# Reordering the banded coefficients of an outlook attention stage by heads, with a copy on ScalarE

## Chip, cores and metric

The kernel runs on one core of a Trainium2 chip, in one launch. The metric is device time in microseconds (us). The kernel before took 2922.51 us, the median of three runs (2905.18, 2922.51 and 2929.6).

The core's engines run side by side, each through its own instructions in a fixed order: TensorE (PE in the profile; its weight loads stand apart as PEld), VectorE (DVE), ScalarE (ACT), GpSimd (POOL) and SyncE (SP), which here issues DMA transfers. A tile of 128 partitions in SBUF is the unit of data; PSUM is where TensorE writes.

## What is computed

The network has two layers on an input of 4 images of 32 x 32 pixels with 384 channels. Layer 0 is a gated attention and a mixture of experts; layer 1 is an "outlook" attention and a feed-forward network whose weights are Kronecker products. The change touches the outlook attention alone. Everything is fp32.

```
v    = x @ Wv                                    # 12 heads of 32 channels
a    = (x @ Wa).reshape(b, n, 12, 9, 9)          # 9 x 9 coefficients for each pixel and head
attn = softmax(a * d ** -0.5, axis=-1)
out[n, h, p] = sum_q attn[n, h, p, q] * v[neighbour q of n, h]   # a 3 x 3 neighbourhood
y    = fold(out)                  # each of the 9 outputs p is added at neighbour p of n
x    = x + y @ Wo
```

Unfolding and folding together mean that the output at a pixel is a weighted sum of v over a 5 x 5 neighbourhood, with one weight for each of 25 offsets and 12 heads.

## The kernel before

**The stage.** `outlook` (L1630) works through 32 tiles of 128 pixels, 8 tiles an image (tile o = 8 b + t). For each tile there are three steps, called at different turns of one loop over 41 steps.

- `scores` (L1721 on), at step o: the normalized tile is transposed on TensorE (`ps_tr`, copied to `xnT` by ScalarE at L151), multiplied by `wa` into 972 coefficients (`ps_a`, L1728, six matmuls of 128x486), turned into a softmax (maximum and subtraction on VectorE, L1737 and L1738; exp on ScalarE, L1743; sums, reciprocal and three multiplications on VectorE, L1745 to L1752), and multiplied by `wv` into `v` (`ps_v` L1772, copied by ScalarE at L1776). Four DMAs on SyncE (L1764 to L1769) move the coefficients of the upper and lower row of the neighbourhood by one image row into the tiles `up` and `down`.
- `band`, at step o + 2: the shifted coefficients are summed in `u` (two ScalarE copies, L1785 and L1786; three VectorE additions), shifted sideways by three matmuls (`ps_c` L1793), masked on VectorE into `co` (L1801), and written by a DMA (L1808, `room<-co`) into a zeroed place in DRAM from which one more DMA (L1814, `band<-room`, 1560 KB) reads a skewed copy: `band[p, t, h]` is the weight with which pixel p of the tile adds to pixel p + t - 66 before or behind it, for t in 0..259 and the 12 heads h. The heads lie innermost.
- `gather`, at step o + 5 (`LAG` is 3): for every head one matmul with `v` of that head as the weights (128 x 32) and `band[:, j : j + n, h]` as the moving operand (128 x n), n being 260, 194 or 66 where an image half cuts the band. Elements of one head are 12 floats (48 bytes) apart. The four heads of a group write four strips of 32 partitions of one PSUM bank, so that four matmuls can run side by side; the three groups have the banks `ys[0]` to `ys[2]`. An image has ten such sets of twelve matmuls, since the tiles t = 3 and t = 4 serve both halves of the image: t = 3 is used once more, with t = 4, when the second half begins. After the last tile of a half, ScalarE copies the three banks to `y` (L1839), and `mix` multiplies by `wo` (`ps_wo` L1846) and adds to x.

**What sets the order.** The order on SyncE and GpSimd is that of the program text. On TensorE, VectorE and ScalarE a scheduler puts the instructions in order when the kernel is built; on the chip each engine keeps to that order. Waits are semaphores that the framework places; a pool's buffer is given again only when its last reader is through. Pools that matter here: `ol_band` (five buffers for `band`; two for `yt`), `ol_ps_m` (two PSUM banks that `ps_tr`, `ps_v` and `ps_wo` share), and one bank each for `ys[0]` to `ys[2]`.

**After the stage** the feed-forward network (`Kron.run`) begins once the last tiles of the last image are mixed.

Of the kernel before, what the change touches and what calls it, by code (L numbers as in the profile page):

```python
# [10 lines left out]
FP = mybir.dt.float32  # L11
# [5 lines left out]
P = 128  # L17
# [4 lines left out]
KC = C // P  # L22
NH, HD = 12, 32
# [18 lines left out]
BAND = P + 2 * REACH  # L42
# [1587 lines left out]
def outlook(net, wv, wa, wo, left, router, kron, loads):  # L1630
# [10 lines left out]
    tc, nc = net.tc, net.nc  # L1641
# [4 lines left out]
    with ExitStack() as ctx:  # L1646
# [2 lines left out]
        mp = ctx.enter_context(tc.tile_pool(name="ol_moved", bufs=4, reuse_waits="tile"))  # L1649
        ap_ = ctx.enter_context(tc.tile_pool(name="ol_attn", bufs=3, reuse_waits="tile"))  # L1650
        vp = ctx.enter_context(tc.tile_pool(name="ol_v", bufs=7, reuse_waits="tile"))
        bp = ctx.enter_context(tc.tile_pool(name="ol_band", bufs=5, reuse_waits="tile"))
        ps_m = ctx.enter_context(tc.tile_pool(name="ol_ps_m", bufs=2, space=PSUM, reuse_waits="tile"))
        ps_a = ctx.enter_context(tc.tile_pool(name="ol_ps_a", bufs=1, space=PSUM, reuse_waits="tile"))
        ps_c = ctx.enter_context(tc.tile_pool(name="ol_ps_c", bufs=1, space=PSUM, reuse_waits="tile"))
# [4 lines left out]
        for dx in (-1, 0, 1):  # L1660
            m = const.tile([P, P], FP, name=f"shift_{dx}", tag=f"shift_{dx}")
# [41 lines left out]
                )  # L1703
            net.measure(work, i, net.x(i))

        attn, vs, bands, ys, moved = {}, {}, {}, {}, {}

        def room(b, t):

# [68 lines left out]
        def band(b, t):  # L1778


            H3 = 3 * H6
            u = work.tile([P, 6, 5, H3], FP, name="u", tag="u")
            down, up = (m.rearrange("p (g y e) -> p g y e", g=6, y=3) for m in moved.pop((b, t)))
            own = attn.pop((b, t))[:, 1].rearrange("p s x (y e) -> p (s x) y e", y=3)
            nc.scalar.copy(u[:, :, 0, :], down[:, :, 0, :])  # L1785
            nc.scalar.copy(u[:, :, 4, :], up[:, :, 2, :])  # L1786
            nc.vector.tensor_tensor(u[:, :, 1:3, :], down[:, :, 1:3, :], own[:, :, 0:2, :], ALU.add)
            nc.vector.tensor_tensor(u[:, :, 3, :], own[:, :, 2, :], up[:, :, 1, :], ALU.add)
            nc.vector.tensor_tensor(u[:, :, 2, :], u[:, :, 2, :], up[:, :, 0, :], ALU.add)
            pc = ps_c.tile([P, 512], FP, name="ps_c", tag="c")  # L1790
            grid = pc[:, : 5 * R].rearrange("p (s y e) -> p s y e", s=2, y=5)
            for qj in (1, 0, 2):
                nc.tensor.matmul(  # L1793
                    grid[:, :, :, (2 - qj) * H6 : (5 - qj) * H6],
                    lhsT=shift[qj - 1],
                    rhs=u.rearrange("p (s x) y e -> p s x y e", s=2)[:, :, qj, :, :],
                    start=qj == 1, stop=qj == 2, skip_group_check=True,
                )
            co = work.tile([P, 5, 5, NH], FP, name="co", tag="co", bufs=3)
            for hh in range(2):  # L1800
                nc.vector.tensor_tensor(  # L1801
                    co[:, :, :, hh * H6 : (hh + 1) * H6],
                    grid[:, hh].rearrange("p y (x h) -> p y x h", x=5),
                    inside.rearrange("p (x h) -> p x h", x=5).unsqueeze(1).to_broadcast([P, 5, 5, H6]),
                    ALU.mult,
                )
            room = net.room[t]
            nc.sync.dma_start(  # L1808
                out=room.rearrange("(p r) -> p r", p=P)[:, : 5 * IMG * NH]
                .rearrange("p (y r) -> p y r", y=5)[:, :, :R],  # L1810
                in_=co.rearrange("p y x h -> p y (x h)"),
            )
            m = bands[b, t] = bp.tile([P, BAND, NH], FP, name="band", tag="band")
            nc.sync.dma_start(  # L1814
                out=m.rearrange("p t h -> p (t h)"),
                in_=room[: P * BAND * NH].rearrange("(p r) -> p r", p=P),
            )

        def gather(b, half, t):

            first, last = (0, 4) if half == 0 else (3, 7)
            lo = max(P * t - REACH, 512 * half)
            hi = min(P * t - REACH + BAND, 512 * half + 512)
            j = lo - (P * t - REACH)
            for c in range(KC):
                if t == first:
                    ys[c] = ps_y.tile([P, 512], FP, name=f"ps_y{c}", tag=f"y{c}")
                for n in range(4):
                    h = 4 * c + n
                    nc.tensor.matmul(  # L1830
                        ys[c][32 * n : 32 * n + 32, lo - 512 * half : hi - 512 * half],
                        lhsT=vs[b, t][:, h * HD : (h + 1) * HD],
                        rhs=bands[b, t][:, j : j + hi - lo, h],
                        start=t == first, stop=t == last, skip_group_check=True,
                    )
            if t == last:
                y = work.tile([P, KC, 512], FP, name="y", tag="y", bufs=1)
                for c in range(KC):
                    nc.scalar.copy(y[:, c, :], ys[c])  # L1839
                return y  # L1840
# [14 lines left out]
        def at(step, f, *args):  # L1855
            later.setdefault(step, []).append((f, args))

        LAG = 3
        made = {}

        def gathered(b, half, t):
            y = gather(b, half, t)
            if y is not None:
                made[b, half] = y
# [4 lines left out]
        for b in range(B):  # L1869
            for t in range(NB):  # L1870
                o = b * NB + t
                at(o + 2, band, b, t)
                at(o + 2 + LAG, gathered, b, 0 if t < 5 else 1, t)
                if t == 4:
                    at(o + 2 + LAG, gathered, b, 1, 3)
                    at(o + 2 + LAG, gathered, b, 1, 4)
            for half in range(2):
                done = b * NB + (4 if half == 0 else 7) + 2 + LAG
                for n in range(4):
                    at(done + 1 + n // 2, mixed, b, half, n)  # L1880
        assert left[0] >= 2 * NB
        t_kron, first = 0, left[0]
        for step in range(B * NB + 9):
            b, t = divmod(step, NB)
# [207 lines left out]
def metaformer_kernel(  # L2092
# [19 lines left out]
    def rest(router, done):  # L2112

        with ExitStack() as late:
# [30 lines left out]
            with tc.manual_schedule(engines={eng.SP, eng.Pool}):  # L2145
                outlook(net, wv, wa, wo, range(done, NT), router, kron, loads)
# [85 lines left out]
```

## Time and profile before

| | |
|---|---|
| median of three runs | 2922.51 us |
| the profiled execution | 2919.42 us, its span 2917.6 us |
| the outlook stage | from about 2340 to 2820 us of the span |
| PE busy | 2761.2 us, 95% |
| DVE, ACT, POOL busy | 1347.7, 1207.3, 400.6 us |
| mean granted TensorE clock | 0.965 |
| banded matmuls (L1830) | 960 records, 102.7 us |

The profile is one execution. A row of a group has the line, the engine, the operation, the tiles written and read, the shapes and the count; then busy time in us, the mean duration of one in ns, and the idle time before them with what ended it. Each fp32 matmul of the program shows as two records, and the durations of matmuls overlap, so that the busy time of a group is less than count times mean. Times of a timeline are us from the span's start.

### The profile page before, as it was taken

How to read it: one execution, taken by the hardware profiler on the slowest of the kernel's cores; microseconds unless marked ns; L12 is line 12 of the kernel's file. 1: busy time of each engine (PE TensorE's matmuls, PEld its weight loads, DVE VectorE, ACT ScalarE, POOL GpSimd, SP SyncE). 2: the span in 40 equal slices, each digit the busy share in tenths (PEclk: the TensorE clock that was granted, in tenths of full speed). 3: DMA queues.
4: the chain of work that ended last, by engine and by line, in shares of the span. 5: the costliest groups of instructions: out<-in, count | busy, mean ns of one | idle time of the engine just before them, and what ended most of it. 6: DMA issues, size and time to landing. Idle time of an engine off the chain costs nothing. (4 is left out here: it accounts for less than half of the span.)

```text
span 2917.6 us, 36735 instructions
## 1 busy us (share of the span) xinstructions
PE 2761.2 (95%) x13236; PEld 1505.9 (52%) x13236; DVE 1347.7 (46%) x3714; ACT 1207.3 (41%) x2023; POOL 400.6 (14%) x499
## 2 busy tenths in 40 slices
PE   6989999999999998699999999999999998999988
PEld 4333333333334332267777777777777754444432
DVE  1376667777777776533000001111111146877642
ACT  3788677677768775211111211211211122122125
POOL 1000000110030004123111122122221101100000
PEclk9999999999999988699999999999999999999999
DMA  5143335223322234345454455555655437544432
GB/s 103 39 115 91 89 90 139 66 62 78 100 55 62 78 79 124 112 163 217 161 195 179 174 203 191 213 201 204 222 190 214 154 130 224 192 154 158 151 105 89
DMA packets 216992, 405.92 MB, mean 139 GB/s; under 512 B 83504, under 2 KB 177904, under 8 KB 203744
## 3 DMA queue, kind: packets, MB, share of 16 engines
q1 hardware_dynamic: 185504, 189.20, 21.6%
q0 software_dynamic: 27152, 209.66, 20.8%
q10 hardware_dynamic: 4144, 4.61, 0.5%
q8 instruction: 107, 1.75, 0.2%
q14 instruction: 85, 0.70, 0.1%
HBM read 305.35 MB, written 49.99 MB: 122 GB/s over the span
## 5 line engine op out<-in xcount | busy, mean ns | idle before, releaser
L1604 ACT ACTIVATE h<-ps_h,up 128x256 f32<-128x256 f32 x420 | 198.6, 473 | 915.2 <-PE ps_h L1600 915.1
L1600 PE MATMUL ps_h<-xbT,up 128*128 128x256 f32 x2520 | 553.2, 380 | 2.6 <-ACT h L1604 1.8
L1617 PE MATMUL ps_y<-down,h 128*128 128x384 f32 x1680 | 554.9, 488 | 0.0
L1600 PEld LDWEIGHTS ps_h<-xbT,up 128*128 128x128 f32 x2520 | 480.7, 191 | 76.7 <-ACT h L1604 2.7
L678 DVE CUSTOM_DVE_ANT_0 e<-e,rz,inv 128x1024 f32<-128x1024 f32 x384 | 475.2, 1274 | 30.0 <-DMA rz<-r_row 30.0
L626 ACT ACTIVATE e<-ps_s,shift 128x1024 f32<-128x1024 f32 x384 | 408.6, 1109 | 81.2 <-PE ps_s L616 48.7
L1617 PEld LDWEIGHTS ps_y<-down,h 128*128 128x128 f32 x1680 | 318.0, 191 | 206.6 <-issue 1.8
L1622 DVE TENSOR_TENSOR y<-ps_y,down 128x384 f32<-128x384 f32 x70 | 39.0, 558 | 721.1 <-PE ps_y L1617 721.1
L616 PE MATMUL ps_s<-q,k 32*128 32x512 f32 x1536 | 279.0, 664 | 36.4 <-ACT e L626 26.7
L634 PE MATMUL ps_o<-e,wv 128*32 128x512 f32 x1536 | 228.4, 670 | 39.3 <-DVE wv L685 36.7
L634 PE MATMUL ps_z<-e,rt_ones 128*32 128x512 f32 x1536 | 218.6, 643 | 0.0
L705 POOL DMA_DIRECT2D q<-po x96 | 76.1, 875 | 958.4 <-DMA q<-po 600.5
L366 ACT ACTIVATE below<-tk_left,tk_bound 128x1024 bf16<-128x1024 f32 (+1 forms) x160 | 184.3, 1152 | 38.0 <-DVE tk_bound L372 31.7
L1728 PE MATMUL ps_a<-wa,xnT 128*128 128x486 f32 x384 | 170.6, 594 | 8.9 <-DVE attn L1738 7.1
L616 PEld LDWEIGHTS ps_s<-q,k 32*128 32x128 f32 x1536 | 84.1, 189 | 168.7 <-ACT e L626 82.6
L281 PE MATMUL ps_t<-xnT,wqkv 128*128 128x512 f32 x288 | 135.4, 611 | 1.1 <-ACT q L520 0.7
L634 PEld LDWEIGHTS ps_o<-e,wv 128*32 128x32 f32 x1536 | 31.7, 112 | 200.3 <-issue 72.6
L1728 PEld LDWEIGHTS ps_a<-wa,xnT 128*128 128x128 f32 x384 | 73.1, 196 | 95.6 <-issue 87.1
L634 PEld LDWEIGHTS ps_z<-e,rt_ones 128*32 128x32 f32 x1536 | 52.7, 118 | 131.1 <-issue 127.1
L1830 PE MATMUL ps_y<-band,v 128*32 128x194 f32 (+2 forms) x960 | 102.7, 516 | 7.2 <-DMA band<-room 6.9
L1569 DVE SCALAR_TENSOR_TENSOR x<-yt,weight,x 128x384 f32<-128x384 f32 x38 | 23.5, 619 | 185.4 <-DMA x<-x 184.7
L1483 POOL DMA_INDIRECT yt<-yg,index x64 | 65.7, 1027 | 304.6 <-DVE x L1569 139.9
(345 smaller groups left out, 2859.2 us busy)
## 6 DMA issues: line engine op xcount, KB each, us to landing
band<-room SPq DMA_DIRECT2D x32, 1560.0 KB
rz<-r_row SPq DMA_DIRECT2D x48, 512.0 KB
yg<-y SPq DMA_DIRECT2D x70, 192.0 KB
q<-q SPq DMA_DIRECT2D x192, 64.0 KB
k<-k SPq DMA_DIRECT2D x192, 64.0 KB
room<-none SPq DMA_DIRECT2D x64, 192.0 KB
x<-x SPq DMA_DIRECT2D x38, 192.0 KB
o<-in_x_dram SPq DMA_DIRECT2D x33, 192.0 KB
```

The lines of the kernel that those rows point to most:

```text
L281: nc.tensor.matmul(ps, lhsT=lhsT(k), rhs=rhs(k), start=k == 0, stop=k == KC - 1)
L366: nc.scalar.activation(junk[:n], left[:n], AF.Sign, bias=bound[:n], accum_out=over[:n])
L616: nc.tensor.matmul(ps[:, half * 512 : half * 512 + 512], lhsT=self.k4[r, u * P : (u + 1) * P], rhs=self.q4[r, :], start=True, stop=True,)
L626: nc.scalar.activation(e, ps, AF.Exp, bias=shift, scale=QK_SCALE)
L634: nc.tensor.matmul(ps[r : r + 32, :], lhsT=lhsT(odd), rhs=self.es[2 * u + odd][:, half * 512 : half * 512 + 512], start=u == 0, stop=u == ...
L678: nc.vector.tensor_tensor_reduce(self.es[m], self.es[m], self.rz, 1.0, self.im["inv"][:, m, self.h : self.h + 1], ALU.mult, ALU.add, self. ...
L705: nc.gpsimd.dma_start(out=there, in_=po[r : r + 32, :], accum_op=ALU.add)
L1600: nc.tensor.matmul(ps, lhsT=up[:, o : o + P], rhs=xbT[:, k, :], start=k == 0, stop=k == KC - 1,)
L1604: nc.scalar.activation(h, ps, AF.Gelu, bias=up[:, KC * HID + f : KC * HID + f + 1])
L1617: nc.tensor.matmul(ps, lhsT=hs[f][:, t * P : (t + 1) * P], rhs=down[:, f * C : (f + 1) * C], start=f == 0, stop=f == NF - 1,)
L1728: nc.tensor.matmul(pa[:, hh, :HW_], lhsT=xnT[:, k, :], rhs=wa[:, k, hh * HW_ : (hh + 1) * HW_], start=k == 0, stop=k == KC - 1,)
L1830: nc.tensor.matmul(ys[c][32 * n : 32 * n + 32, lo - 512 * half : hi - 512 * half], lhsT=vs[b, t][:, h * HD : (h + 1) * HD], rhs=bands[b, t ...
```

## The change

ScalarE copies each landed band into a second tile `own` in which the heads are outermost, and the banded matmuls read that. The copy is three instructions, one for each group of four heads, of 4 x 260 = 1040 elements in each partition: it reads elements 48 bytes apart and writes elements that lie side by side. In the program text it stands at step o + 4, one before the gather. The buffers change with it: three for the landed band (five before) and two for the copy. `sort` stands at L1819 to L1825 of the changed kernel; what follows it moves down by eight or nine lines (the banded matmul is L1838 there).

```diff
-        bp = ctx.enter_context(tc.tile_pool(name="ol_band", bufs=5, reuse_waits="tile"))
+        bp = ctx.enter_context(tc.tile_pool(name="ol_band", bufs=1, reuse_waits="tile"))
...
-            m = bands[b, t] = bp.tile([P, BAND, NH], FP, name="band", tag="band")
+            m = landed[b, t] = bp.tile([P, BAND, NH], FP, name="band", tag="band", bufs=3)
...
+        def sort(b, t):
+
+            m = landed.pop((b, t))
+            own = bands[b, t] = bp.tile([P, NH, BAND], FP, name="own", tag="own", bufs=2)
+            for c in range(KC):
+                heads = slice(4 * c, 4 * c + 4)
+                nc.scalar.copy(own[:, heads, :], m[:, :, heads].rearrange("p t h -> p h t"))
...
-                        rhs=bands[b, t][:, j : j + hi - lo, h],
+                        rhs=bands[b, t][:, h, j : j + hi - lo],
...
                 at(o + 2, band, b, t)
+                at(o + 1 + LAG, sort, b, t)
                 at(o + 2 + LAG, gathered, b, 0 if t < 5 else 1, t)
```

More of the change, by code (lines that the diff above doesn't have):

```diff
@@ L1704, in add @@
             net.measure(work, i, net.x(i))
-        attn, vs, bands, ys, moved = {}, {}, {}, {}, {}
+        attn, vs, landed, bands, ys, moved = {}, {}, {}, {}, {}, {}
         def room(b, t):
```

## The prediction

> **What bounds the kernel now.** I read first the busy time by stretches of the span, to see which engine the outlook stage waits for; its columns are the stretch, its length, then for PE, PEld, DVE, ACT and POOL the busy us and instructions, the clock, DMA share and GB/s.
>
> ```profile
> 2460.00:2500.00 40.00, 38.40 (x207) 20.09 (x200) 31.91 (x80) 10.38 (x18) 9.83 (x10) 1.00 0.76 231
> ...
> 2580.00:2620.00 40.00, 40.00 (x200) 19.68 (x199) 27.27 (x67) 7.10 (x14) 0.00 (x0) 1.00 0.46 156
> 2620.00:2660.00 40.00, 40.00 (x165) 19.37 (x160) 28.51 (x72) 8.64 (x18) 0.72 (x2) 1.00 0.47 157
> 2660.00:2700.00 40.00, 40.00 (x232) 19.69 (x224) 29.63 (x82) 12.00 (x22) 0.00 (x0) 1.00 0.46 153
> ...
> 2780.00:2820.00 40.00, 32.33 (x238) 16.01 (x236) 17.37 (x44) 6.85 (x12) 0.00 (x0) 0.91 0.50 173
> ```
>
> From 2540 to 2784 TensorE never idles, VectorE works 70% and ScalarE 20% to 30%. There a shorter matmul shortens the stage. At both ends TensorE idles: transfers and chains bound it.
>
> Second, the groups of instructions by shape, from 2420 to 2815 (the last row is from the page's list of groups):
>
> ```profile
> L1846 PE MATMUL ps_wo<-wo,y 128*128 128x384 f32 x168 | 57.7, 491 | 0.0
> ...
> L1830 PE MATMUL ps_y<-band,v 128*32 128x260 f32 x384 | 56.1, 628 | 2.8 <-DMA band<-room 2.8
> ...
> L150 PE MATMUL ps_tr<-ident,xn 128*128 128x128 f32 x75 | 12.7, 276 | 0.7 <-DVE x L1850 0.7
> ...
> L1830 PE MATMUL ps_y<-band,v 128*32 128x66 f32 x192 | 8.8, 295 | 0.2 <-ACT y L1839 0.2
> ...
> L634 PE MATMUL ps_o<-e,wv 128*32 128x512 f32 x1536 | 228.4, 670 | 39.3 <-DVE wv L685 36.7
> ```
>
> A banded column costs (628 - 295) / (260 - 66) = 1.72 ns; a column that streams side by side (491 - 276) / (384 - 128) = 0.84 ns. The last row, of the same 128*32 form but contiguous, takes 670 ns for 512 columns, where 1.72 ns a column would make some 1060. So the 48-byte step is the cause, and it costs a factor of 2.05.
>
> Third, the timeline of ScalarE and SyncE around one tile, and the chain of waits at the end:
>
> ```profile
> 2597.22 1.01 ACT L1743 ACTIVATE attn<-attn 128x972 f32<-128x972 f32 x1 [0.47 <-DVE attn L1738]
> ...
> 2613.16 1.01 ACT L1743 ACTIVATE attn<-attn 128x972 f32<-128x972 f32 x1 [0.25 <-DVE attn L1738]
> 2619.66 0.48 ACT L151 COPY xnT<-ps_tr 128x384 f32<-128x384 f32 x1 [5.48 <-PE ps_tr L150]
> ```
>
> ```profile
> 2620.03 0.54 SPq L1764 DMA_DIRECT2D up<-attn  x1
> ...
> 2622.57 0.53 SPq L1808 DMA_DIRECT2D room<-co  x1
> 2624.99 0.33 SPq L1814 DMA_DIRECT2D band<-room  x1
> ```
>
> ```profile
> 2807.64 6.32 DMA band<-room
> 2814.00 2.22 PE ps_y L1830 x24
> ```
>
> The exp of a tile ends at 2614.17; SyncE issues that tile's moves at 2620.03, behind them the band of two tiles before at 2624.99, and a band lands 6.32 us after its issue: 2631.3, 17.1 us after the exp. This loop matters below.
>
> **The change part by part.** All sums are made against the profiled execution, 2919.42 us (its span 2917.6 and 1.8 around it), 0.1% under the median of the three runs.
>
> TensorE. The four strips of a set run side by side, so a run of banded matmuls lasts as long as its fullest strip. In the built order of before there are 48 such runs with 53,504 columns in the fullest strips (two records a matmul): 92.0 us at 1.72, and the remaining 10.7 of the measured 102.7 are 0.22 a run for starting and draining. In the built order of the changed kernel the scheduler cuts the sets elsewhere: 56 runs, 55,188 columns. At 0.84 and 0.22 that is 46.4 + 12.3 = 58.7 us; 44 us or 43% of the banded work goes. Between 2540 and 2784 it was 63.8 us, so 27.4 there. That stretch holds 206 / 12 = 17.2 tiles (twelve records of `ps_a` each): 14.2 us a tile, which would become 12.6.
>
> ScalarE gains three copies of 128x1040 for each of 32 tiles. No row shows it reading SBUF in steps of 48 bytes. From below: 1024 elements side by side from SBUF take 1054 ns (L359), so 1040 take 1.07 us. From above: 0.2 us fixed (1054 less 1024 x 0.83, the slope between its 384- and 512-element copies) and TensorE's 1.72 ns an element, 2.0 us. I take 2.0: TensorE reads the same bytes in the same steps, which is nearest, and pays.
>
> Here the Trainium skill speaks on both sides. "ScalarE: Activation LUTs", in its section on the ACT_TABLE_LOAD cost, gives one element a cycle, 0.83 ns, without a word on steps; by it the copies take 1.07 us and the sum below comes to 2888. "SBUF — State Buffer", in the section on SBUF's two sides, says that an access in a new 16-byte line each time pays a penalty, in the memory and not in one engine; that agrees with the factor 2.05 here and speaks against the change, whose copies pay what the matmuls are spared. "Vector Engine (DVE) Microarchitecture Reference", 5.2, gives 2.50 ns an element for small steps on VectorE; by an estimate from it a copy takes 2.8 us and the sum is near 2950. No run here shows either.
>
> What the copy delays. ScalarE has room (at most 12 of 40 us busy), but it is one queue. In the changed order, for most tiles, the copies of tile o stand after `xnT` of tile o + 4 and ahead of two `u` copies, the `v` copy and the exp of tile o + 4. Should the band not have landed, all of these wait. So a loop of two tiles closes: exp of o + 2, 17.1 us to the landing, 6.0 of copies, 1.9 for the four behind them (0.28 + 0.18 + 0.48 + 1.01), next exp: 25.0 us, 12.5 a tile. That equals TensorE's 12.6; two equal paces whose steps vary (tiles with and without `ps_wo`, 3.9 us) lose to each other. I put 0.4 a tile for that: (14.2 - 12.6 - 0.4) x 17.2 = 21 us gained.
>
> Two buffers of `own`. Tile t = 3 is read until the second half's first set, and t = 5 needs its buffer. In the changed order two copies follow that set, then the exp, the third copy and `xnT`, before the next score matmuls: 3 x 2.0 + 1.0 + 0.5 = 7.5 us, where TensorE has some 3.8 of other work (sets of 66 and 194 columns, `ps_c`, `ps_tr`, the next set). 3.7 lost for each of two images in this stretch: -7.
>
> Early tiles (2403 to 2460). The copies stand there between an exp (end 2413.66) and the `u` copies, which ran at once; `ps_c` ran at 2417.6. With 6.0 between, `u` is done about 2420.0: 2.4 lost a tile against 1.1 gained on a set of 194. Two or three tiles pay before the wait on VectorE at 2450 (2.75 us) swallows it: -3. From 2460 to 2540 TensorE idles for transfers too; of 6.7 us saved (43% of 15.6) I count half: +3.
>
> The end. After the landing at 2814.0 come three copies, then the `y` copies, since ScalarE's order has them last: 6.0 + 0.6 + 0.1 to the first `ps_wo`, 2.1 before: -4.6. The sets there waited for bands; their saving is worth nothing.
>
> With one answer: three landed buffers cost nothing as a band's transfer waits for the copies of three tiles before, done a tile earlier; were they not, SyncE would stand, and with it the next moves. The DMAs are the same in number and order. VectorE's 10 us a tile fit in 12.6.
>
> Sum: +21 - 7 - 3 + 3 - 4.6 = 9.4 us gained: 2910.
>
> **The rivals.**
>
> A, the copies run at the contiguous price, 1.07 us. The loop is 17.1 + 3.2 + 1.9 = 22.2, 11.1 a tile, so TensorE paces: +27.4; buffers -2, early +3, middle +5, end -1.8: 2919.4 - 31.6 = 2888. For it: the exp and the copies show 0.83 ns an element. Against it: none of them steps.
>
> B, slower: ScalarE's queue becomes the pace of the stage. The loop decides it: 2 x 14.2 - 17.1 - 1.9 = 9.4 us for three copies, 3.1 each, and the early tiles already lose from 2.0. If ScalarE pays the excess of the step twice (0.83 + 2 x 0.88 = 2.6 ns), a copy takes 2.9: the loop 27.7, 13.9 a tile, gains 5; the buffers take (8.7 + 1.5 - 3.8) x 2 = 13; early, `ps_c` is 5.1 late against 1.1, four for each of six tiles, 24; the end 7.3. Together -39: 2958. For it: no cover in the queue at the early tiles. Against it: no row is that slow.
>
> C, the matmuls don't get faster, since four strips at once were the limit and not the step. Then the copies only cost: 3 x 2.4 at the early tiles, 7 for the buffers, 4.6 at the end: 2938. Against it stands the L634 row.
>
> **How the numbers follow.** Main case 0.55 (2910, 2890 to 2930 by its own unknowns), A 0.18, B 0.19, C 0.08. 1% is about what a measurement tells from no change: 2890 and 2949. Faster takes most of A and a tail of the main case, 0.16; slower most of B, 0.16; the rest, 0.68, is the same. The range reaches through A's middle and most of B: 2884 to 2955.
>
> **What would show it.** The banded group should take 55 to 62 us busy, its 260-column records some 400 ns. A copy row of 128x1040 near 2.0 us confirms the step's price for ScalarE; near 1.07 gives A, near 2.9 gives B. TensorE should then idle between 2540 and 2784, for `xnT`, `v` or the copies, by some 15 us, and some 6 to 7 us should pass between the last landing and the last `ps_wo`. Wrong I would be if SyncE stood on landed buffers, if other transfers slowed, or if ScalarE's strided reads slowed the matmuls that run beside them.

## The result, and the profile after

The changed kernel took 2917.61 us, the median of ten runs (2911.0 to 2920.11); the kernel before, beside it on the same chip, 2917.93. The ratio is 0.9998, with a 95% interval of 0.9981 to 1.0015: no change that can be measured. Its profiled execution has a span of 2918.4 us, against 2917.6.

So two things that each show plainly in the profile, faster matmuls and new copies, cancel. To see where, I cut the outlook stage at the first `ps_a` matmul of some tiles (o from 0 to 31) and at the first matmul of the feed-forward network that follows. Only lengths are compared, since what stands ahead of the stage shifts by tens of us from chip to chip. Each row is one profiled execution, in us:

| run | o = 1 to 8 | 8 to 14 | 14 to 31 (a tile) | 31 to the network | stage |
|---|---|---|---|---|---|
| before | 79.7 | 84.5 | 238.8 (14.04) | 52.9 | 455.8 |
| after | 80.0 | 90.4 | 227.8 (13.40) | 57.9 | 456.1 |

By these cuts the steady stretch gained 11.0 us; the middle tiles lost 5.9, the end 5.0, the first tiles 0.3. But the cut at o = 14 doesn't part the same work. In the built order of the changed kernel 18 records of the banded matmuls and six of `ps_c` stand ahead of it, from 2537.82 to 2541.77, that stood behind it before:

```profile
2537.82 1.08 PE L1838 MATMUL ps_y<-own,v 128*32 128x260 f32 x16
2540.20 0.62 PE L1838 MATMUL ps_y<-own,v 128*32 128x260 f32 x2 [1.29 <-DVE xf L1971]
```

They are 2.7 us of TensorE's work, so that some 8.3 us of the 11.0 are gained and some 3.2 of the 5.9 are lost. Both kernels have the same 1724 records from o = 1 to 31, and these took 403.0 and 398.2 us.

A row is one execution, too. The kernel before, e10 and e11 below run the same instructions in the same order from o = 1 to 8, and took 79.7, 78.1 and 80.8 us: a difference of 2 or 3 us between two rows tells little by itself.

What the change did to its two operations stands in the groups. From the page's list of groups:

```profile
L1825 ACT COPY own<-band 128x1040 f32<-128x1040 f32 x96 | 191.1, 2050 | 35.4 <-DMA band<-room 35.4
```

and by shape, from 2420 to 2815:

```profile
L1838 PE MATMUL ps_y<-own,v 128*32 128x260 f32 x384 | 34.8, 403 | 14.1 <-ACT own L1825 12.8 <-DVE xf L1971 1.3
...
L1838 PE MATMUL ps_y<-own,v 128*32 128x194 f32 x376 | 25.9, 357 | 3.1 <-ACT own L1825 3.1
...
L1838 PE MATMUL ps_y<-own,v 128*32 128x66 f32 x192 | 7.9, 260 | 5.8 <-ACT own L1825 5.8
```

A banded record of 260 columns fell from 628 ns to 403, and a copy takes 2050 ns. The last part of each row is what changed: before, 7.2 us stood idle ahead of the banded matmuls, nearly all for landings, and now 23 us do (14.1 + 3.1 + 5.8), nearly all until a copy to `own` was through. The stretches that the prediction showed of before are now (the columns are its: length, then PE, PEld, DVE, ACT, POOL, the clock, DMA share, GB/s):

```profile
2460.00:2500.00 40.00, 30.40 (x173) 16.03 (x174) 28.20 (x74) 20.69 (x22) 9.62 (x10) 0.87 0.75 223
2580.00:2620.00 40.00, 36.71 (x183) 18.53 (x182) 26.23 (x62) 23.93 (x23) 0.00 (x0) 0.91 0.47 154
2620.00:2660.00 40.00, 39.40 (x182) 21.26 (x180) 31.59 (x80) 26.18 (x27) 0.72 (x2) 1.00 0.50 165
2660.00:2700.00 40.00, 34.63 (x231) 18.71 (x232) 30.66 (x85) 29.75 (x32) 0.00 (x0) 1.00 0.48 155
...
2780.00:2820.00 40.00, 27.55 (x187) 13.98 (x188) 13.84 (x37) 28.68 (x22) 0.00 (x0) 0.70 0.42 140
```

TensorE, full in the middle rows before, now has gaps there, and the clock is no longer 1.00 everywhere. ScalarE works up to 30 of 40 us and no longer 7 to 12. At the end the chain of waits has a new link:

```profile
2802.68 6.29 DMA band<-room
2809.07 6.02 ACT own L1825 x3
2815.14 0.87 PE ps_y L1838 x8
2816.01 3.94 PE ps_wo L1854 x6
```

The last band lands, three copies run one after the other, TensorE waits for each, and `ps_wo` starts 7.0 us after the landing instead of 2.2.

### The profile page after: what moved, and what is told of

Read it like the earlier page. It is cut to its first block, busy times and chain, and to the rows that moved or that the text cites. A ratio compares the mean times of both kernels' runs of the same rounds, so it can differ in the third digit from the quotient of the medians.

```text
span 2918.4 us, 36837 instructions
## 1 busy us (share of the span) xinstructions
PE 2729.3 (94%) x13236; PEld 1497.4 (51%) x13236; DVE 1348.0 (46%) x3714; ACT 1392.5 (48%) x2119; POOL 401.0 (14%) x499
## 5 line engine op out<-in xcount | busy, mean ns | idle before, releaser
L626 ACT ACTIVATE e<-ps_s,shift 128x1024 f32<-128x1024 f32 x384 | 408.6, 1109 | 84.5 <-PE ps_s L616 45.1
L1825 ACT COPY own<-band 128x1040 f32<-128x1040 f32 x96 | 191.1, 2050 | 35.4 <-DMA band<-room 35.4
L1728 PE MATMUL ps_a<-wa,xnT 128*128 128x486 f32 x384 | 172.0, 598 | 13.4 <-ACT xnT L151 7.5
L634 PEld LDWEIGHTS ps_z<-e,rt_ones 128*32 128x32 f32 x1536 | 53.3, 119 | 134.6 <-issue 130.5
```

The source lines that it names most:

```text
L626: nc.scalar.activation(e, ps, AF.Exp, bias=shift, scale=QK_SCALE)
L634: nc.tensor.matmul(ps[r : r + 32, :], lhsT=lhsT(odd), rhs=self.es[2 * u + odd][:, half * 512 : half * 512 + 512], start=u == 0, stop=u == ...
L1728: nc.tensor.matmul(pa[:, hh, :HW_], lhsT=xnT[:, k, :], rhs=wa[:, k, hh * HW_ : (hh + 1) * HW_], start=k == 0, stop=k == KC - 1,)
L1825: nc.scalar.copy(own[:, heads, :], m[:, :, heads].rearrange("p t h -> p h t"))
```

## Where the gain of the steady stretch goes

One number splits that stretch. Its length, TensorE's busy time and the clock, first before, then of the changed kernel, from o = 14 to 31:

```profile
2535.40:2774.20 238.80, 238.75 (x1087) 116.69 (x1088) 172.60 (x439) 53.46 (x105) 5.24 (x8) 1.00 0.48 158
```

```profile
2541.80:2769.60 227.80, 214.29 (x1064) 113.85 (x1063) 168.22 (x424) 152.34 (x156) 5.27 (x8) 0.98 0.49 161
```

The kernel before was busy for 238.75 of its 238.8 us. Two of the experiments below (e5 and e9), which have the changed kernel's matmuls here at a clock of 1.00, are busy for 210.0. That is 28.7 us less, of which 2.7 are the 24 records that stand ahead of the cut; e1 below, with all 1087 records, shows 27.6 for the shorter matmuls alone. Of the 28.7, 13.5 are lost as idle time and 4.3 as a slower clock (214.3 less 210.0). TensorE's waits there, with the sum in us, the times and the longest:

```profile
PE ps_y L1838 <- ACT own L1825: 7.4, 5, 2.2
PE ps_a L1728 <- ACT xnT L151: 3.2, 4, 1.9
PE ps_v L1772 <- ACT xnT L151: 2.0, 2, 1.2
```

The first row is mostly the two buffers. The timeline of TensorE (start, us, and in brackets the idle time before) at t = 5 of an image:

```profile
2587.11 0.65 PE L1838 MATMUL ps_y<-own,v 128*32 128x260 f32 x8
2588.87 0.65 PE L1838 MATMUL ps_y<-own,v 128*32 128x260 f32 x8 [1.12 <-ACT own L1825]
2591.69 1.07 PE L1838 MATMUL ps_y<-own,v 128*32 128x260 f32 x2 [2.17 <-ACT own L1825]
2592.69 7.64 PE L1728 MATMUL ps_a<-wa,xnT 128*128 128x486 f32 x12
```

The three groups of heads come one copy at a time, and 3.3 us are lost. The next image loses 1.28 and 2.18 at the same place. Here the six score matmuls that follow also take 7.64 us instead of 5.16: the clock was down.

The other two rows come from ScalarE's queue. A copy waits for its band to land, and `xnT` of a later tile stands behind it (ScalarE's timeline):

```profile
2621.68 2.07 ACT L1825 COPY own<-band 128x1040 f32<-128x1040 f32 x1 [3.74 <-DMA band<-room]
2623.66 0.48 ACT L151 COPY xnT<-ps_tr 128x384 f32<-128x384 f32 x1
```

## The experiments

My theory before them: the copies' price decides, by a loop of exp, landing and copies that paces the steady stretch, by two buffers, and by the chain at the end. The rivals: ScalarE's busy time is the pace whatever the order; or the new order of TensorE's work and not the copies takes the gain back. Each group of runs was compared with the kernel before on its own chip (2952.64 us for e1 to e4, 2924.78 for e5 to e8, 2953.13 for e9 to e11, 2952.91 for e12). The stage lengths of all of them:

| run | o = 1 to 8 | 8 to 14 | 14 to 31 (a tile) | 31 to the network | stage | time, us | ratio to before |
|---|---|---|---|---|---|---|---|
| e1_no_copy | 78.2 | 85.8 | 213.2 (12.54) | 52.1 | 429.3 | 2924.24 | 0.9891 (0.9855 to 0.9926) |
| e2_copies_only | 81.5 | 96.5 | 236.1 (13.89) | 55.1 | 469.1 | 2965.52 | 1.0043 (1.0018 to 1.0068) |
| e3_flat_copy | 75.5 | 91.5 | 213.1 (12.54) | 52.7 | 432.8 | 2925.83 | 0.9922 (0.9891 to 0.9952) |
| e4_pairs | 77.4 | 90.0 | 214.7 (12.63) | 53.3 | 435.3 | 2932.0 | 0.9924 (0.9896 to 0.9952) |
| e5_own3 | 80.3 | 92.4 | 220.5 (12.97) | 58.4 | 451.6 | 2915.42 | 0.9977 (0.9956 to 0.9999) |
| e6_lag4 | 78.8 | 81.4 | 234.3 (13.78) | 63.9 | 458.5 | 2917.76 | 0.9992 (0.997 to 1.0015) |
| e7_pairs_own3 | 77.6 | 93.4 | 211.8 (12.46) | 53.6 | 436.3 | 2894.34 | 0.9899 (0.9869 to 0.9929) |
| e8_four_copies | 81.5 | 96.7 | 231.1 (13.59) | 60.4 | 469.7 | 2938.71 | 1.0057 (1.0036 to 1.0077) |
| e9_behind_xnT | 80.2 | 91.4 | 217.6 (12.80) | 58.4 | 447.6 | 2939.55 | 0.9969 (0.9943 to 0.9995) |
| e10_pairs_some | 78.1 | 83.0 | 218.2 (12.84) | 51.0 | 430.3 | 2925.37 | 0.9912 (0.9885 to 0.994) |
| e11_late | 80.8 | 84.0 | 230.1 (13.53) | 57.2 | 452.1 | 2952.96 | 0.9997 (0.9969 to 1.0024) |
| e12_vector_order | 79.8 | 92.7 | 231.2 (13.60) | 58.0 | 461.6 | 2955.72 | 1.0013 (0.9985 to 1.0041) |

**The matmuls alone (e1_no_copy).** The kernel before, with the landed bytes read as if the heads were outermost.

```diff
-            m = bands[b, t] = bp.tile([P, BAND, NH], FP, name="band", tag="band")
+            m = bands[b, t] = bp.tile([P, NH, BAND], FP, name="band", tag="band")
...
-                        rhs=bands[b, t][:, j : j + hi - lo, h],
+                        rhs=bands[b, t][:, h, j : j + hi - lo],
```

> The banded matmuls stream side by side with no copy at all: the landed tile is read as if the heads were outermost, so which coefficient meets which pixel is left out (five buffers as before). Theory 1 (ScalarE's copies, 5.9 us a tile in its one queue, give back what TensorE gains): nothing is left to give back, the banded group takes 55 to 60 us busy and the time falls by 27 to 35 us, to 2883 to 2891. Theory 2 (transfers or VectorE pace the stage at some 14 us a tile whatever TensorE does): within 6 us of the kernel before, 2918.

The stage fell by 26.5 us, 25.6 of them in the steady stretch (14.04 to 12.54 a tile). From o = 1 to 14 it took 164.0 us, before 164.2: shorter matmuls are worth nothing there.

**The copies alone (e2_copies_only).** The kernel before, with the three copies of each band into a scratch tile that nobody reads.

```diff
+        def sort(b, t):
+            m = bands[b, t]
+            own = bp.tile([P, 4, BAND], FP, name="own", tag="own", bufs=1)
+            for c in range(KC):
+                heads = slice(4 * c, 4 * c + 4)
+                nc.scalar.copy(own, m[:, :, heads].rearrange("p t h -> p h t"))
...
+                at(o + 1 + LAG, sort, b, t)
```

> The copies alone: ScalarE makes the three strided copies of each landed band into a scratch tile that nobody reads, and the matmuls read the landed band as before. Theory 1: only the cost is left; the time rises by 15 to 30 us, to 2933 to 2948, with TensorE idle between 2540 and 2784. Theory 2: the copies lie beside other work, within 6 us of 2918.

In the steady stretch a tile took 13.89 us, no more than before; the cost lies between o = 8 and 14 (12.0, of which some 2 are 16 banded records that stand ahead of the cut here) and at both ends (1.8 and 2.2). TensorE's strided records didn't mind the strided copies beside them, 628 ns before and here:

```profile
L1838 PE MATMUL ps_y<-band,v 128*32 128x260 f32 x384 | 56.2, 628 | 2.1 <-DMA band<-room 2.1
```

**The price of the step (e3_flat_copy, e4_pairs).** e3 is the changed kernel with copies that read and write side by side, so that the order by heads is left out. e4 keeps the computation whole: the heads are copied in pairs, and the matmuls read one word of each pair, in steps of 8 bytes.

```diff
-                nc.scalar.copy(own[:, heads, :], m[:, :, heads].rearrange("p t h -> p h t"))
+                nc.scalar.copy(
+                    own[:, heads, :].rearrange("p h t -> p (h t)"),
+                    m.rearrange("p t h -> p (t h)")[:, 4 * c * BAND : 4 * (c + 1) * BAND],
+                )
```

> The changed kernel with the copies reading side by side: each of the three moves 1040 elements as they lie, so the order by heads is left out; their number, place, buffers and waits stay. The step's price alone is taken away. Theory 1: a copy takes 1.07 us, three 3.1; the loop of exp, band, copy, exp falls below TensorE's pace, and the time falls to 2885 to 2895. Theory 2: a copy takes 1.07 us, and the time stays within 6 us of 2918. If a copy still takes 2 us, the step is not what it pays for.

```diff
-            own = bands[b, t] = bp.tile([P, NH, BAND], FP, name="own", tag="own", bufs=2)
+            own = bands[b, t] = bp.tile([P, NH // 2, BAND, 2], FP, name="own", tag="own", bufs=2)
...
-                nc.scalar.copy(own[:, heads, :], m[:, :, heads].rearrange("p t h -> p h t"))
+                nc.scalar.copy(
+                    own[:, 2 * c : 2 * c + 2], m[:, :, heads].rearrange("p t (g e) -> p g t e", e=2)
+                )
...
-                        rhs=bands[b, t][:, h, j : j + hi - lo],
+                        rhs=bands[b, t][:, h // 2, j : j + hi - lo, h % 2],
```

> The copy goes into an order by pairs of heads: it reads two neighbouring words at a time, and the matmuls read every second word (8 bytes apart). The right result. If a read pays for a step only when each word lies apart from the last (two neighbours are free), copies take 1.1 us and matmuls 0.84 ns a column: theory 1 gives 2885 to 2895, theory 2 2918. If any step costs the same, copies take 2 us and the matmuls 1.7 ns a column: 2930 to 2940 by theory 1.

The copy group of e3:

```profile
L1825 ACT COPY own<-band 128x1040 f32<-128x1040 f32 x96 | 95.9, 1056 | 58.0 <-DMA band<-room 53.6 <-PE ps_wo L1857 4.4
```

and, of e4, the copy and the banded groups:

```profile
L1825 ACT COPY own<-band 128x1040 f32<-128x1040 f32 x96 | 102.3, 1125 | 55.7 <-DMA band<-room 52.5 <-PE ps_y L1840 3.2
...
L1840 PE MATMUL ps_y<-own,v 128*32 128x260 f32 x384 | 33.6, 399 | 4.2 <-ACT own L1825 3.5 <-DVE a_rows L1746 0.7
```

A copy takes 1056 ns side by side, 1125 by pairs, 2050 by single words. TensorE reads one word of each pair as fast as contiguous words (399 against 403 ns). From o = 1 to 31 both runs have TensorE's and ScalarE's instructions in the changed kernel's order, and with short copies the steady stretch is 14.7 and 13.1 us shorter (12.54 and 12.63 a tile). So in this stretch the duration of a copy decides, not that there is one, nor the new order of TensorE's work.

**Two buffers (e5_own3).** The changed kernel with three buffers for `own` and two for the landed band.

```diff
-            m = landed[b, t] = bp.tile([P, BAND, NH], FP, name="band", tag="band", bufs=3)
+            m = landed[b, t] = bp.tile([P, BAND, NH], FP, name="band", tag="band", bufs=2)
...
-            own = bands[b, t] = bp.tile([P, NH, BAND], FP, name="own", tag="own", bufs=2)
+            own = bands[b, t] = bp.tile([P, NH, BAND], FP, name="own", tag="own", bufs=3)
```

> The changed kernel with three buffers of the copy and two of the landed band (instead of two and three), so that no copy waits for the last reader of tile t = 3. The stage is timed from the score matmuls of the second tile to the first matmul of the network after it: 455.7 us before the change, 456.1 after. If the two buffers cost what was forecast, 449 to 451 here; if the wait for the buffer lies in a time in which ScalarE would wait for the landing anyway (the loop of exp, band, copies, exp takes 26.6 us for two tiles in the changed kernel), 453 to 457.

The steady stretch gained 7.3 us. Its row, and TensorE's waits there:

```profile
2543.00:2763.40 220.40, 210.03 (x1064) 112.53 (x1062) 167.28 (x423) 152.10 (x156) 5.28 (x8) 1.00 0.51 166
```

```profile
PE ps_a L1728 <- ACT xnT L151: 6.6, 6, 2.6
PE ps_v L1772 <- ACT xnT L151: 1.7, 2, 0.9
PE ps_y L1838 <- ACT own L1825: 1.2, 2, 1.0
```

The waits for `own` went from 7.4 to 1.2; but those for `xnT` grew from 5.2 to 8.3, so that the idle time fell by 3.1 only. The other 4.2 came back as clock, 0.98 to 1.00. The whole stage is 4.5 us shorter, since the other stretches took 2.8 more.

**A step more between landing and gather (e6_lag4).** `LAG` 4 instead of 3, one more buffer for `v`, one more turn of the loop.

```diff
-        LAG = 3
+        LAG = 4
```

> The changed kernel with LAG = 4: copy and gather come one step later (one more buffer for v), so that on ScalarE the copies of tile o stand, for most tiles, behind the exp of o + 4, and the loop goes over three tiles; the copies still take 2.05 us and ScalarE is as busy. If the loop sets the pace, TensorE takes over: 12.5 to 12.9 us a tile from the 15th to the last instead of 13.4, the stage 440 to 447 us. If ScalarE is simply too busy, the pace and the stage stay, 453 to 460.

Inconclusive. The copies hardly waited for landings, but with the two buffers held a step longer TensorE waited more for `own` (8.3 us of the steady stretch) and `xnT` (9.3), and the end took 63.9 us. Two things moved at once. (Its o = 8 to 14 is short, 81.4 us, because with the gathers a step later only 351 matmul records lie in it, where the changed kernel has 403.)

**Pairs and three buffers (e7_pairs_own3).** The edits of e4 and e5 together.

> The order by pairs of heads (copies near 1.1 us) with three buffers of the copy and two of the landed band. With short copies neither loop nor buffer should bind: the stage within 3 us of the 435.3 us that pairs with two buffers took, 20 us under the kernel before.

The stage took 436.3 us, as e4's 435.3: with short copies, the third buffer had little left to give.

**One copy more (e8_four_copies).** The changed kernel with a fourth copy of 2.05 us for each tile, into a scratch tile.

```diff
+            more = bp.tile([P, 4, BAND], FP, name="more", tag="more", bufs=1)
+            nc.scalar.copy(more, m[:, :, 0:4].rearrange("p t h -> p h t"))
```

> The changed kernel with a fourth copy of the same kind for each tile, into a scratch tile that nobody reads: 2 us more in ScalarE's queue. If the loop over two tiles sets the pace, each tile takes 1.0 us longer from the 15th to the last (14.3 to 14.5), and the stage takes 475 to 490 us with early tiles and end. If ScalarE's whole work per tile sets it, 2.05 us longer (15.4), the stage 495 to 510. If the copies are hidden, no change, 455 to 460.

In 14 of the 17 tiles of the steady stretch it stands directly behind the three. This run felled part of my theory. If the loop of two tiles were the pace, a tile would have become 1 us longer; if ScalarE's busy time were, 2 us. It became 0.19 longer (13.40 to 13.59). The loop had slack, so the loss in the steady stretch is local: single places where something TensorE needs stands in ScalarE's queue behind copies. Of the 13.6 us that its stage is longer, 7.8 fell before o = 14 and 2.5 at the end, where there is no cover.

**The copies behind `xnT` (e9_behind_xnT).** e5, with the copies of tile o tied behind the `xnT` of tile o + 4 in ScalarE's order.

```diff
-                nc.scalar.copy(own[:, heads, :], m[:, :, heads].rearrange("p t h -> p h t"))
+                with tc.issue_after(turned[min(b * NB + t + 4, NT - 1)]):
+                    nc.scalar.copy(own[:, heads, :], m[:, :, heads].rearrange("p t h -> p h t"))
```

> As e5_own3 (three buffers for own, two for the landed band), and the copies of tile o are tied behind the xnT copy of tile o + 4 in ScalarE's order; nothing is left out. Theory (what is left of the loss in the steady stretch is the xnT copy standing behind a copy that itself waits for its band to land): TensorE's waits for xnT, 8.3 us between tiles 15 and 32 in e5, fall under 2 us, the clock dips that follow them go too, and a tile takes 12.5 to 12.75 us there (e5: 12.97); the stage takes 445 to 448 us (e5: 451.6), the ratio is some 0.996. Rival (the sum of landing, copies and exp is the pace, whatever the order): the waits reappear as ps_y waiting for own, and a tile stays at 12.97 and the stage at 451.

Half a hit. The order alone gained 2.9 us (12.97 to 12.80 a tile; the stage 447.6), so `xnT` behind a landing is a cause:

```profile
PE ps_a L1732 <- ACT xnT L1726: 4.4, 3, 1.9
PE ps_v L1776 <- ACT xnT L1726: 1.6, 2, 0.8
PE ps_y L1843 <- ACT own L1830: 1.4, 2, 1.3
```

But 6.0 us of waits for `xnT` are left, where I had expected under 2. In ScalarE's timeline the three of `ps_a` stand behind an exp that was itself late: twice after copies (one of them 4.03 us late for its band), once after a wait for VectorE. With copies of 1.1 us such waits nearly end (e4: 1.2 us); which link of the queue to move next was not tried.

**No copies for the first nine tiles (e11_late).** The changed kernel; for o < 9 the banded matmuls read the landed band in steps of 48 bytes, as before (every second one of these lands in a buffer of `own`, which makes five for them).

```diff
+        def plain(b, t):
+            o = b * NB + t
+            return o < 9
...
-                at(o + 1 + LAG, sort, b, t)
+                if not plain(b, t):
+                    at(o + 1 + LAG, sort, b, t)
```

> The changed kernel with one thing undone: the first nine of the 32 tiles are not copied, their banded matmuls read the landed band in steps of 48 bytes as before; nothing is left out. Theory (the 5.9 us lost over the middle tiles 9 to 15 come from copies that stand ahead of the u copies and the exp in ScalarE's queue while transfers leave TensorE idle): tiles 2 to 15 take 164 to 166 us instead of 170.4, the steady stretch stays at 13.4 us a tile, the end at 57.9, the stage at some 450 us, ratio 0.997 to 0.999. Rival (the middle loses for another reason, such as where the scheduler puts the matmuls, or transfers that start at other times): tiles 2 to 15 stay at 169 to 171 us and the stage at 456, ratio 1.000.

(The expectations of e9 to e11 count tiles from 1; "tiles 2 to 15" is o = 1 to 14 here.) From o = 1 to 14 it took 164.8 us, not 170.4. Of these 5.6 us, 2.7 are the 24 records, which stand behind the cut here as before. One execution is thin ground, but more runs have this stretch: without copies in it 161.1 to 164.8 us (before, e1, e10, e11; mean 163.5), with long ones 170.4 to 172.7 (after, e5, e9, e12; mean 171.8), with short ones 167.0 to 171.0 (e3, e4, e7; mean 168.5). Less the 24 records, long early copies cost some 5.6 us and short ones some 2.3. The stage of e11 took 452.1; the interval around its ratio, 0.9997, is too wide to tell these 4 us. From o = 8 to 14, first the changed kernel, then e11:

```profile
2451.40:2541.80 90.40, 77.02 (x404) 40.23 (x405) 71.20 (x180) 60.90 (x61) 12.48 (x14) 0.94 0.64 194
```

```profile
2483.00:2567.00 84.00, 78.81 (x379) 39.50 (x379) 65.99 (x166) 19.38 (x38) 13.02 (x14) 0.96 0.62 191
```

TensorE has 13.4 us without work in the one, 5.2 in the other. The theory's mechanism doesn't tell all: e3 and e4, whose copies take half the time, are 4.5 and 2.6 us sooner at o = 8, but need 91.5 and 90.0 us here. The largest single gap is on TensorE (first fence), and VectorE's timeline (second) says why:

```profile
2475.02 0.94 PE L1793 MATMUL ps_c<-u,shift 128*128 128x180 f32 x2 [5.70 <-DVE u L1789]
```

```profile
2472.67 0.62 DVE L1701 SCALAR_TENSOR_TENSOR x<-yt,weight,x 128x384 f32<-128x384 f32 x1 [4.63 <-DMA yt<-yg,index]
...
2474.61 0.26 DVE L1789 TENSOR_TENSOR u<-u,up 128x108 f32<-128x108 f32 x1
```

L1701 adds rows that small gathers of layer 0's output bring (`yt`, two buffers, issued by GpSimd). With the copies in the early tiles the scheduler put one L1701 ahead of the outlook's own additions; it waits 4.63 us for its gather, and they and `ps_c` wait with it. Without early copies VectorE has the order of before.

**VectorE's order (e12_vector_order).** So the changed kernel once more, with three of these L1701 tied behind the outlook's operations, where before had them.

```diff
+        behind = {13: ("u", 7), 20: ("mul", 10), 22: ("mul", 14)}
...
+                added.append(n)
+                after = behind.get(len(added))
+                with tc.issue_after(passed[after]) if after else nullcontext():
+                    nc.vector.scalar_tensor_tensor(
```

> The changed kernel with all its copies; only VectorE's order is tied at three places of the middle tiles (o = 8 to 14): three of the additions x<-yt,weight,x (L1701), which wait for small gathers that GpSimd issues, are put behind the outlook's own additions and multiplications, as they stood in the kernel before. Nothing is left out. The changed kernel takes 90.4 us from o = 8 to 14 and idles 5.7 us there for u, whose addition stands behind such an L1701 that waits 4.6 us for its gather; e3 and e4, with copies of half the length, show the same wait and the same 90 to 91.5 us; e1, e10 and e11 have the order of before. Theory (the middle tiles lose by the place of L1701 in VectorE's order, which the scheduler moved): the wait of 5.7 us is gone, o = 8 to 14 takes 84 to 87 us, the steady stretch stays at 13.4 a tile and the end at 58, the stage is some 451 us, the ratio 0.997 to 1.000. Rival (the time that copies take in ScalarE's queue ahead of u and exp): o = 8 to 14 stays at 89 to 92 us and the stage at 455 to 457.

A miss. The wait of 5.70 us for `u` was gone, and o = 10 followed o = 9 after 11.6 us instead of 18.6; but o = 8 to 14 took 92.7 us all the same: the next L1701 waited 4.01 and 4.47 us for their gathers, and behind them `ps_tr` idled:

```profile
2522.47 0.90 PE L150 MATMUL ps_tr<-ident,xn 128*128 128x128 f32 x3 [6.66 <-DVE x L1863]
```

VectorE's waits for `yt` from o = 8 to 14 sum to 4.2 us before, 4.7 in e11 and 5.3 in e10; to 10.3 after, 10.7 in e12, 8.9 and 9.5 in e3 and e4, and 10.8 in e1. In e1, with VectorE's order of before, they grew as the matmuls shrank, and in e12 moving one wait moved the loss. But the sums don't follow the length: e8 has only 6.3 and, with 96.7 us, the longest stretch; there TensorE waited 7.5 us for `u` behind ScalarE's copies. So the gathers and ScalarE's queue both take part. Shown is that early copies cost time, the long ones more than the short; by which link, and whether they make the gathers late, stays open.

**Pairs where they pay (e10_pairs_some).** e4, with no copy for o < 9 and for the last two tiles, whose matmuls read the landed band directly.

```diff
+            return o < 9 or o >= 30
...
-                        rhs=bands[b, t][:, h // 2, j : j + hi - lo, h % 2],
+                        rhs=bands[b, t][:, j : j + hi - lo, h] if plain(b, t)
+                        else bands[b, t][:, h // 2, j : j + hi - lo, h & 1],
```

> The copy of e4 (heads in pairs) for tiles 9 to 29 alone; for the first nine and the last two of the 32 tiles the banded matmuls read the landed band in steps of 48 bytes, as in the kernel before; nothing is left out. Theory (the copies cost where ScalarE's queue or the last chain is exposed, and the shorter matmuls are worth something only in the steady stretch): tiles 2 to 15 take 162 to 165 us (before 164.2, after 170.4, e4 167.4), a tile of the steady stretch 12.6 us, the end 52.5 us (before 52.9, after 57.9), the stage some 430 us, 26 under before: ratio 0.989 to 0.992, the best of the versions that compute everything. Rival (what is lost in the middle tiles comes from the change of pace there and not from the copies): tiles 2 to 15 take 167 us or more and the stage stays near 435.

The stage took 430.3 us, 25.5 under before and within a us of e1, which has no copies at all. From o = 1 to 14 it took 161.1, the end 51.0; the steady stretch, at 12.84 a tile, came 0.24 over what I had expected (some 0.15 of it are the 24 records, which e4 has ahead of the cut at o = 14 and e10 behind it). Of all that compute everything this has the shortest stage, but by the ratios (0.9912 here, 0.9899 for e7, 0.9924 for e4) the three are not told apart.

## Why the prediction was right, and where it was not

The forecast, 2910 and no measurable change, holds: 2917.61, the ratio 0.9998. But the 9.4 us of gain that the sum has did not come: it holds because the sum was small and its range wide (2884 to 2955). Four terms held in size, a fifth (the loop) is there by another mechanism, one step failed, and a loss of 4.3 us by the clock has no term at all.

**TensorE.** 27.4 us were to go between 2540 and 2784; e1, with the same records in the steady stretch, shows 27.6, the changed kernel 28.7, of which 2.7 moved ahead of the cut. The banded group as a whole missed its mark: 68.6 us busy (34.8 + 25.9 + 7.9) where 55 to 62 were foretold; e1 has 60.2 (31.9, 23.2 and 5.1 by shape). The two hardly differ in the steady stretch (33.7 and 33.5 us). They do in the middle tiles (13.8 at a clock of 0.94, 10.3 in e1, which has 18 records fewer there) and at the end (14.7 at 0.79, 10.7 in e1), where the sets wait between copies, are cut into shorter runs, and meet a lower clock.

**ScalarE's price.** 2.0 us taken, 2.05 measured; with it rivals A (1.07) and B (2.9) fall. Rival C falls by the 403 ns. The rule of the Trainium skill, "SBUF — State Buffer", in the section on SBUF's two sides, that an access in a new 16-byte line each time pays a penalty, agrees with both engines here: 2050 against 1056 ns, a factor of 1.94 for ScalarE beside 2.05 for TensorE. The 0.83 ns an element of "ScalarE: Activation LUTs" holds for e3 ((1056 - 200) / 1040 = 0.82, with the working's fixed 200 ns), nearly for e4 (0.89), and not for the step (1.78); and an estimate from VectorE's 2.50 ns ("Vector Engine (DVE) Microarchitecture Reference", 5.2) would have been wrong by 0.8 us a copy.

**Two buffers.** -7 by the sum; e5 gained 7.3 in the steady stretch. The place was right too: two waits for copies of t = 5 in each of two images, 3.3 and 3.5 us against 3.7 foretold. Of the 7.3, though, 4.2 came as clock. And SyncE never stood on a landed buffer: its waits before `band<-room` are for `room<-co` alone.

**The loop.** "Two equal paces whose steps vary lose to each other", 0.4 a tile or 6.9 us. A loss of that order is there (in e5, 10.4 us of idle time), but not by that mechanism: e8 lengthened the loop by 2.05 us in two tiles, and the pace changed by 0.19 a tile instead of 1.0. In its place stand single waits for `xnT` (e9) behind copies and what follows them. With the 24 records put back the steady stretch gained some 8.3 us where the sum had 14. The idle time came out as priced (13.5 against 6.9 + 7); 4.3 of what is short is clock.

**First and middle tiles.** This step failed. -3 for the first and +3 for 2460 to 2540 made 0; it was -0.3 and, with the 24 records put back, some -3.2 (by the means of the groups under e11, -5.6 for both). The +3 was wrong: that half of the shorter matmuls would count in the middle was an assumption, and e1, without copies, gained nothing there (164.0 us against 164.2). The -3 for the copies was near in size but not in place: I had priced them by what stands behind them in ScalarE's queue, up to the wait on VectorE at 2450, and at nothing from there on, and it is there that they cost. What the sum doesn't have at all are VectorE's waits for the `yt` gathers, 4.2 us before and 10.3 after, which take part in that loss; VectorE's old order (e12) did not give it back.

**The end.** -4.6 by the sum, 5.0 measured: 6.02 of copies and the first `ps_wo` 7.0 us after the landing, the working's 6.7. (The list of what would show it said the last `ps_wo`; the working is about the first.)

Together the sum was 9.7 us too good: 0.4 at the end, and the rest, with the 24 records put back, some 5.7 in the steady stretch and some 3.5 at the first and middle tiles (by the cut as it stands 3.0 and 6.2).

## What to carry to other kernels

A copy that puts strided data in order pays the step that it spares the reader; before adding one, look for an order by pairs of words: ScalarE read them in 1125 ns against 2050 here (1056 side by side), and TensorE read one word of each pair at full rate. An engine with much room in its busy time is not cover for a long instruction: what counts is what stands behind it in that queue, and at which places the engine that paces the stage waits for that. Such a copy was worth its time here in the stretch where the shorter work sets the pace, and not where the stage fills and drains: without it there, e10's stage was 5 us shorter than e4's, though the times themselves do not tell the two apart. And before two stretches are compared, count the instructions in each: a scheduler can move work across the cut.

## What the runs showed of the hardware

A short wait of TensorE can cost about as much again in clock. After the 1.12 and 2.17 us shown above, this stretch follows:

```profile
2592.00:2600.00 8.00, 8.00 (x14) 3.33 (x13) 1.96 (x5) 6.42 (x7) 0.00 (x0) 0.64 0.40 103
```

The granted clock is 0.64, and the score matmuls take 2.5 us longer. After the like pair of waits of the next image (1.28 and 2.18 us) they ran at full speed. The Trainium skill, "TensorE: Matmul & The Clock Gate", Part 1, has the clock fall after an idle window of about 3.4 us that runs free of the work; that a like pause may or may not be hit agrees with a free-running window, but here the pause was broken, with 0.65 us of matmuls between two waits of 3.3 us in sum. Further on a single wait of 1.90 us, well short of that window, was followed by 3.4 us at a clock of 0.50 (from 2730.84), while e5 kept 1.00 through waits of up to 2.6 us.

Strided reads of SBUF by ScalarE and TensorE at the same time did not slow each other: in e2 a copy took 2041 ns (2050 beside contiguous matmuls) and a banded record 628 (628 without copies). Of the 384 records of 260 columns in e2, 158 lie wholly inside a copy, and these took 630 ns.
